# Order of the bilinear blends on VectorE: both columns of a pair, then both rows

## The chip, the cores and the metric

The kernel runs on one core of a Trainium2 chip. The metric is the device time of one execution in microseconds (us). Before the change it is 6806.22 us, the median of 10 runs (6788.82 to 6811.57).

The core's engines work in parallel, each through its own instructions in a fixed order, and wait for one another by semaphores: TensorE (PE in the profile; PEld are its weight loads), VectorE (DVE), ScalarE (ACT), GpSimd (POOL) and SyncE (SP). GpSimd issues the indirect transfers here, SyncE most of the plain ones.

## The reference

An image batch x of shape (4, 256, 64, 64), float32, goes through one block: three modulated deformable 3x3 convolutions with ReLU on the channel-normalised x, a residual, then a mixture of 8 experts (two per token) on the normalised tokens, and another residual. The change lies in the sampling of the deformable convolutions:

```python
def _bilinear(feat, ys, xs):
    y0 = jnp.floor(ys)
    x0 = jnp.floor(xs)
    wy = (ys - y0)[:, None]
    wx = (xs - x0)[:, None]
    ...
    return v00 * (1 - wy) * (1 - wx) + v01 * (1 - wy) * wx + v10 * wy * (1 - wx) + v11 * wy * wx

def _deform_layer(x, w_off, b_off, w, b, dilation=1):
    om = lax.conv_general_dilated(x, w_off, ...) + b_off[None, :, None, None]
    off = om[:, :2 * K].reshape(B, K, 2, H, W)
    mask = jax.nn.sigmoid(om[:, 2 * K:])
    ...
    sampled = _bilinear(x, ys, xs) * mask[:, None]
    wk = w.reshape(w.shape[0], w.shape[1], K)
    out = jnp.einsum('bikhw,oik->bohw', sampled, wk) + b[None, :, None, None]
    return out
```

Every output position has K = 9 taps, and every tap is one bilinear sample of all 256 channels at a position that the offset convolution gives.

## The kernel before

**Tiling.** An image is cut into 8 blocks of 512 positions (4 groups of 128). Three layers times four images make 12 stages; in each the loop of `main_block` runs over 8 blocks, 9 taps and 2 pairs of groups. A pair is two samples of 128 positions by 256 channels. That makes 12 x 8 x 9 x 2 = 1728 pairs and 3456 samples.

**One sample** (`samples`, lines 494 to 519). GpSimd issues an indirect transfer (L503) that gathers, for each of 128 positions, the four corner pixels with 256 channels each, from a table in DRAM into a tile `g` of shape 128 x 2 x 2 x 256. VectorE blends twice. L509, called the columns here, blends the two corners of each of the two columns (512 numbers a partition, with one coefficient of `cf`, in place in `g`). L514, called the rows, blends the two results across (256 numbers, with another coefficient), out of `g` into a tile `s`. The second reads what the first has just written. ScalarE then scales `s` with the third coefficient, which holds the mask and the corner weight (L517).

**One pair further** (`turn`, `finish`). Two pairs later in the program (`LAG = 2`), TensorE transposes the pair's two samples by 128x128 blocks into `tp` (L532), ScalarE copies them to `sT` (L535), and once both pairs of a tap are there, TensorE multiplies them by the tap's weights into `acc` (L555).

**Buffers.** `g` has 10 buffers (`GB`), given back when the rows are blended. `s` has 8 (`smp`), given back when the sample is transposed. A gather or a blend of rows whose buffer is not free waits, and all that stands behind it on its engine waits too.

**Work beside it.** `step` and `pump` put the other work between the taps in pieces: the offset convolution and the sampling plan of the next layer (`off_block`, L357 to L427), the normalisation of the next image (`pre_block`, L442 to L467; its last operation on VectorE is L78), tokens and routing, and the experts (`expert`, L840 to L874, with weights fetched by L800 and tokens by L812; `products` L892; `combine` L915 and L930; `give` L948).

**What sets the order.** The program is not run as written: at build time a scheduler runs a model of the program and fixes each engine's order by readiness and by place in the program. Where the author wants an order, `after(x)` adds the condition that the instructions traced inside it are issued behind `x` on the same engine. `self.last` holds the newest blend of rows, and work beside it on VectorE is often put behind that one.

Of the kernel before, what the change touches and what calls it, by code (L numbers as in the profile page):

```python
# [11 lines left out]
ALU = mybir.AluOpType  # L12
# [105 lines left out]
class Weave:  # L118
# [375 lines left out]
    def samples(self, i, n, k, t0, plan):  # L494


        nc = self.nc
        idx, cf = plan
        ss = []
        for t in (t0, t0 + 1):  # L500
            j = t * K + k
            g = self.gat.tile([P, 2, 2, C], F32, tag="g", name=f"g_{i}_{n}_{j}")
            self.gathered = nc.gpsimd.indirect_dma_start(  # L503
                out=g.rearrange("p x s f -> p (x s f)"),
                out_offset=None,
                in_=self.table(*self.stages[i]),
                in_offset=bass.IndirectOffsetOnAxis(ap=idx[:, j : j + 1], axis=0),
            )
            nc.vector.scalar_tensor_tensor(  # L509
                g[:, :, 0, :], g[:, :, 1, :], cf[:, j, 0:1], g[:, :, 0, :],  # L510
                ALU.mult, ALU.add,
            )
            s = self.smp.tile([P, C], F32, tag="s", name=f"s_{i}_{n}_{j}")
            self.last = nc.vector.scalar_tensor_tensor(  # L514
                s, g[:, 1, 0, :], cf[:, j, 1:2], g[:, 0, 0, :], ALU.mult, ALU.add
            )
            nc.scalar.activation(s, s, AF.Copy, scale=cf[:, j, 2:3])  # L517
            ss.append(s)
        return ss
# [616 lines left out]
```

## Time and profile before

| what | value |
| --- | --- |
| median of 10 runs | 6806.22 us |
| the profiled execution | 6797.38 us |
| its span, first to last instruction | 6795.6 us |
| mean granted clock of TensorE | 0.978 |
| columns, L509: count, busy, mean | 3456, 2558.8 us, 742 ns |
| rows, L514: count, busy, mean | 3456, 1659.9 us, 482 ns |
| scale, L517 (ScalarE): count, busy, mean | 3456, 1642.0 us, 508 ns |
| copy to sT, L535 (ScalarE): count, busy, mean | 1728, 1001.3 us, 586 ns |
| gather, L503 (GpSimd): count, busy, mean | 3456, 3646.5 us, 1055 ns |
| products, L555 (TensorE): count, busy | 6912, 3383.4 us |
| transposes, L532 (TensorE): count, busy | 6912, 1255.2 us |
| DMA, gathers and other indirect transfers | 1947.35 MB, 77.9% of 16 engines' span |

The busy shares of the engines over the span, in 40 equal slices (each digit in tenths, 9 is 90% or more):

```profile
PE   7998888889999999999999999999998899988987
DVE  7887778778999676668889777677778555688521
ACT  3554555555555445445555444545554444454322
POOL 4664766666667666666667777666666666677643
DMA  8998999999999999999998999989998888899744
```

The busy time of an engine counts only work; time in which it stands at a wait is idle, and the profile names what ended it. The chain of waits goes back from the last instruction, at each step to what released it or to the instruction ahead of it on its engine; its shares tell which engine's work lay on the path that set the end. A matmul's end is modelled, so a busy TensorE may still hold small gaps.

### The profile page before, as it was taken

The numbers are of one execution on the slowest core, as the hardware profiler recorded it, in microseconds if no ns is written. First come the engines' busy times: TensorE is split into PE (matmuls) and PEld (weight loads), VectorE is DVE, ScalarE is ACT, GpSimd is POOL, SyncE is SP. The second block draws the span as 40 slices with busy tenths as digits, with TensorE's granted clock in tenths as the row PEclk, the third lists the DMA queues.
The fourth block names the chain that finished last, engine by engine and source line by source line (L and its number), as shares of the span: only waits on it lengthen the run. The fifth ranks groups of instructions, "written<-read, shape, count | busy, mean of one in ns | idle before, by whom it ended". The sixth has DMA issues, their size and how long they took to land.

```text
span 6795.6 us, 88985 instructions
## 1 busy us (share of the span) xinstructions
PE 6215.6 (91%) x26500; PEld 3527.7 (52%) x26500; DVE 4961.4 (73%) x11467; ACT 3283.2 (48%) x7141; POOL 4443.5 (65%) x4245
## 2 busy tenths in 40 slices
PE   7998888889999999999999999999998899988987
PEld 3443344444445555555554545555555566755675
DVE  7887778778999676668889777677778555688521
ACT  3554555555555445445555444545554444454322
POOL 4664766666667666666667777666666666677643
PEclk8999999999999999999999999999999999999998
DMA  8998999999999999999998999989998888899744
GB/s 290 349 352 300 367 354 369 357 349 388 382 393 351 330 349 336 321 338 347 356 364 309 357 355 383 320 326 344 346 341 325 282 287 276 291 350 339 249 138 125
DMA packets 800319, 2223.73 MB, mean 327 GB/s; under 512 B 104728, under 2 KB 302872, under 8 KB 794080
## 3 DMA queue, kind: packets, MB, share of 16 engines
q0 software_dynamic: 551200, 1947.35, 77.9%
q1 hardware_dynamic: 248640, 270.69, 11.8%
q8 instruction: 215, 3.52, 0.2%
q14 instruction: 264, 2.16, 0.1%
HBM read 2160.68 MB, written 196.40 MB: 347 GB/s over the span
## 4 chain that ended last, share of the span: by engine, by line
PE 71%; ACT 8%; DMA 6%; DVE 6%; issue 4%; POOL 3%; SPq 0%; ACTq 0%; DVEq 0%; POOLq 0%
PE acc L555 36%; PE tp L532 10%; PE ph L856 7%; PE py L874 7%; PE po L357 7%; DMA g<-tab,idx 5%; ACT sT L535 3%; DVE g L509 2%; ACT s L517 2%; DVE s L514 2%; POOL gy L915 1%; POOL g L503 1%; PE pm L371 1%; PE ftp L840 1%; ACT win L577 1%
## 5 line engine op out<-in xcount | busy, mean ns | idle before, releaser
L503 POOL DMA_INDIRECT g<-tab,idx x3456 | 3646.5, 1055 | 1803.7 <-DVE s L514 655.0
L555 PE MATMUL acc<-sT,wk 128*128 128x512 f32 x6912 | 3383.4, 603 | 151.8 <-ACT sT L535 137.1
L509 DVE SCALAR_TENSOR_TENSOR g<-g,cf 128x512 f32<-128x512 f32 x3456 | 2558.8, 742 | 404.4 <-DMA g<-tab,idx 400.3
L514 DVE SCALAR_TENSOR_TENSOR s<-g,cf 128x256 f32<-128x256 f32 x3456 | 1659.9, 482 | 751.0 <-PE tp L532 466.9
L535 ACT COPY sT<-tp 128x512 f32<-128x512 f32 x1728 | 1001.3, 586 | 1823.8 <-PE tp L532 1819.1
L517 ACT ACTIVATE s<-s,cf 128x256 f32<-128x256 f32 x3456 | 1642.0, 508 | 449.5 <-DVE s L514 411.5
L555 PEld LDWEIGHTS acc<-sT,wk 128*128 128x128 f32 x6912 | 1161.2, 192 | 964.9 <-issue 653.5
L532 PEld LDWEIGHTS tp<-ident,s 128*128 128x128 f32 x6912 | 882.7, 143 | 1359.9 <-issue 652.4
L532 PE MATMUL tp<-ident,s 128*128 128x128 f32 x6912 | 1255.2, 281 | 195.4 <-ACT s L517 178.7
L856 PE MATMUL ph<-fzT,w 128*128 128x256 f32 x2608 | 689.4, 397 | 56.2 <-ACT fzT L844 36.1
L874 PE MATMUL py<-w,hT 128*128 128x256 f32 x2608 | 653.6, 389 | 30.4 <-ACT hT L866 26.8
L856 PEld LDWEIGHTS ph<-fzT,w 128*128 128x128 f32 x2608 | 485.4, 197 | 184.4 <-ACT fzT L844 63.7
L874 PEld LDWEIGHTS py<-w,hT 128*128 128x128 f32 x2608 | 475.3, 192 | 162.6 <-ACT hT L866 70.0
L866 ACT ACTIVATE hT<-ph,w 128x256 f32<-128x256 f32 x652 | 282.2, 471 | 446.1 <-PE ph L856 426.9
L812 POOL DMA_INDIRECT zt<-z,tok x326 | 334.5, 1026 | 156.5 <-issue 84.9
L357 PE MATMUL po<-win,wo 128*32 128x504 f32 (+1 forms) x2304 | 354.9, 594 | 5.9 <-ACT win L301 3.6
L800 POOL DMA_INDIRECT w<-in_W,wrow x163 | 177.1, 1086 | 270.3 <-issue 101.7
L915 POOL DMA_INDIRECT gy<-ys,slots x256 | 261.6, 1022 | 102.5 <-issue 66.0
L892 DVE TENSOR_TENSOR y<-py,w 128x512 f32<-128x512 f32 x163 | 111.5, 684 | 225.8 <-PE py L874 225.8
L930 DVE SCALAR_TENSOR_TENSOR ta<-gy,cw,ta 128x256 f32<-128x256 f32 x256 | 120.4, 479 | 123.8 <-DMA gy<-ys,slots 77.7
L357 PE MATMUL po<-win_pre,wo 128*32 128x504 f32 (+1 forms) x1152 | 185.9, 622 | 2.0 <-ACT om L366 2.0
L357 PEld LDWEIGHTS po<-win,wo 128*32 128x32 f32 x2304 | 72.7, 109 | 176.0 <-issue 140.3
(154 smaller groups left out, 2929.1 us busy)
## 6 DMA issues: line engine op xcount, KB each, us to landing
tab<-hv SPq DMA_DIRECT2D x512, 128.0 KB, 7.2
g<-tab,idx POOLq DMA_INDIRECT x3456
ys<-y SPq DMA_DIRECT2D x163, 256.0 KB, 4.5
tab<-h_pre SPq DMA_DIRECT2D x128, 256.0 KB, 6.5
wk<-in_conv_w SPq DMA_DIRECT2D x99, 256.0 KB, 7.6
xc_pre<-in_x SPq DMA_DIRECT2D x32, 512.0 KB, 8.3
xr_tok<-in_x SPq DMA_DIRECT2D x32, 512.0 KB, 8.4
t<-t_tok SPq DMA_DIRECT2D x32, 512.0 KB, 6.2
```

Source lines behind the costliest of these rows:

```text
L357: nc.tensor.matmul(po[g * Q : (g + 1) * Q, :].rearrange("q (r w) -> q r w", w=W)[:, :, x0:x1], lhsT=self.wo[l][:, 3 * ky + kx, c, :], rhs= ...
L503: self.gathered = nc.gpsimd.indirect_dma_start(out=g.rearrange("p x s f -> p (x s f)"), out_offset=None, in_=self.table(*self.stages[i]), ...
L509: nc.vector.scalar_tensor_tensor(g[:, :, 0, :], g[:, :, 1, :], cf[:, j, 0:1], g[:, :, 0, :], ALU.mult, ALU.add,)
L514: self.last = nc.vector.scalar_tensor_tensor(s, g[:, 1, 0, :], cf[:, j, 1:2], g[:, 0, 0, :], ALU.mult, ALU.add)
L517: nc.scalar.activation(s, s, AF.Copy, scale=cf[:, j, 2:3])
L532: self.turned = nc.tensor.transpose(tp[:, c, u * P : (u + 1) * P], ss[u][:, c * P : (c + 1) * P], self.ident)
L535: nc.scalar.copy(self.sT[:, :, t0 * P : (t0 + 2) * P], tp)
L555: nc.tensor.matmul(acc[:, o, :], lhsT=self.wk[k][:, c, o * P : (o + 1) * P], rhs=sT[:, c, :], start=(k == 0 and c == 0), stop=(k == K - 1 ...
L812: self.nc.gpsimd.indirect_dma_start(out=zt, out_offset=None, in_=grp.zd, in_offset=bass.IndirectOffsetOnAxis(ap=grp.tok[:, j : j + 1], axi ...
L856: nc.tensor.matmul(ph[:, h, :], lhsT=w1[:, o : o + P], rhs=zT[:, c, :], start=(c == 0), stop=(c == CC - 1),)
L874: nc.tensor.matmul(py[:, u, :], lhsT=hT[h // 2][:, h % 2, u * P : (u + 1) * P], rhs=w2[:, h * C : (h + 1) * C], start=(h == 0), stop=(h == ...
L915: self.nc.gpsimd.indirect_dma_start(out=g, out_offset=None, in_=self.ys[grp.i % 3], in_offset=bass.IndirectOffsetOnAxis(ap=grp.slots[:, i, ...
```

## The change

In `samples`, the loop over the two samples of a pair is split in two. The first loop gathers and blends the columns of each sample; the second blends the rows and scales. The rows of both samples are put behind the columns of the second (`newest` is the last one that the first loop made). No operation is added or removed, and no shape changes.

```diff
-        ss = []
+        ss, gs = [], []
         for t in (t0, t0 + 1):
             j = t * K + k
             g = self.gat.tile([P, 2, 2, C], F32, tag="g", name=f"g_{i}_{n}_{j}")
...
-            nc.vector.scalar_tensor_tensor(
+            newest = nc.vector.scalar_tensor_tensor(
                 g[:, :, 0, :], g[:, :, 1, :], cf[:, j, 0:1], g[:, :, 0, :],
                 ALU.mult, ALU.add,
             )
+            gs.append((j, g))
+        for j, g in gs:
             s = self.smp.tile([P, C], F32, tag="s", name=f"s_{i}_{n}_{j}")
-            self.last = nc.vector.scalar_tensor_tensor(
-                s, g[:, 1, 0, :], cf[:, j, 1:2], g[:, 0, 0, :], ALU.mult, ALU.add
-            )
+            with self.after(newest):
+                self.last = nc.vector.scalar_tensor_tensor(
+                    s, g[:, 1, 0, :], cf[:, j, 1:2], g[:, 0, 0, :], ALU.mult, ALU.add
+                )
             nc.scalar.activation(s, s, AF.Copy, scale=cf[:, j, 2:3])
             ss.append(s)
         return ss
```

## The prediction

> **What bounds the kernel now.** I read the page's busy line and its chain first, to see whose time sets the end.
>
> ```profile
> PE 6215.6 (91%) x26500; PEld 3527.7 (52%) x26500; DVE 4961.4 (73%) x11467; ACT 3283.2 (48%) x7141; POOL 4443.5 (65%) x4245
> ...
> PE 71%; ACT 8%; DMA 6%; DVE 6%; issue 4%; POOL 3%; SPq 0%; ACTq 0%; DVEq 0%; POOLq 0%
> PE acc L555 36%; PE tp L532 10%; PE ph L856 7%; PE py L874 7%; PE po L357 7%; DMA g<-tab,idx 5%; ACT sT L535 3%; DVE g L509 2%; ACT s L517 2%; DVE s L514 2%; POOL gy L915 1%; POOL g L503 1%; PE pm L371 1%; PE ftp L840 1%; ACT win L577 1%
> ```
>
> TensorE is busy 91% of the span and holds 71% of the chain. VectorE, the engine that the change works on, holds 6%. The two blends (L509 the columns, L514 the rows) are 2% each.
>
> Second, the timeline of VectorE alone, in a stretch that happens to hold both orders (start, duration, line; x2 is two in a row):
>
> ```profile
> 2001.02 1.40 DVE L509 SCALAR_TENSOR_TENSOR g<-g,cf 128x512 f32<-128x512 f32 x2
> 2002.35 0.87 DVE L514 SCALAR_TENSOR_TENSOR s<-g,cf 128x256 f32<-128x256 f32 x2
> 2003.14 0.74 DVE L509 SCALAR_TENSOR_TENSOR g<-g,cf 128x512 f32<-128x512 f32 x1
> 2004.01 0.48 DVE L514 SCALAR_TENSOR_TENSOR s<-g,cf 128x256 f32<-128x256 f32 x1
> 2004.41 0.75 DVE L509 SCALAR_TENSOR_TENSOR g<-g,cf 128x512 f32<-128x512 f32 x1
> 2005.29 0.48 DVE L514 SCALAR_TENSOR_TENSOR s<-g,cf 128x256 f32<-128x256 f32 x1
> ```
>
> A blend that reads the operation just ahead starts 0.13 us after it (2003.14 + 0.74 = 2003.88, next at 2004.01). One that reads nothing of it starts 0.07 us before its end (2002.42 against 2002.35). The first pair, in the order that the change asks for, takes 2.20 us (2001.02 to 2003.22), the second 2.63 us (2003.14 to 2005.77). So the stall exists, and the new order removes 0.43 us a pair.
>
> Third, TensorE's waits and those of VectorE and GpSimd on this path (total us, times, longest us).
>
> ```profile
> PE tp L532 <- ACT s L517: 178.7, 278, 2.9
> PE acc L555 <- ACT sT L535: 137.1, 209, 2.1
> ...
> PE tp_pre L462 <- DVE h_pre L78: 36.5, 15, 5.3
> ```
>
> ```profile
> DVE s L514 <- PE tp L532: 466.9, 544, 5.0
> DVE g L509 <- DMA g<-tab,idx: 400.3, 274, 10.8
> ```
>
> ```profile
> POOL g L503 <- DVE s L514: 655.0, 549, 14.0
> ```
>
> TensorE's waits for a sample are for its scale on ScalarE (L517). I followed each one back in the records: if the scale began more than 0.12 us after its blend of rows had ended, ScalarE's own queue was the cause, otherwise what held the blend. Of 183 us so followed, 141 us are ScalarE's queue, 26 us a gather that landed late, 5 us a blend that itself waited for TensorE, and only 11.5 us VectorE's queue. VectorE loses more time waiting for TensorE to give back a sample buffer (466.9 us) than TensorE loses waiting for VectorE. In 558 of the 659 such waits the buffer is that of the sample eight before: the ring of 8 is full.
>
> **The change part by part.** Nothing is added or removed: 3456 blends of columns, 3456 of rows, as many scales and gathers. The gathers keep their order in the program. What moves is the first sample's blend of rows, behind the second's blend of columns, and with it the first scale.
>
> *The stall.* Counting VectorE's records, 1783 blends of rows begin 0.10 to 0.17 us after their own blend of columns with nothing between; in the median the gap is 0.133 us, against -0.081 us behind other work. That makes 1783 x 0.214 = 382 us off VectorE's queue. On the path it is little: the chain holds 81 such neighbours, 26 of them behind a blend that a late gather let go. Those 26 lose in the new order (next part), so 55 x 0.214 = 12 us are gained. The other 1702 lie under TensorE's work. The waits for the normalised block (L78, 15 times) gain too: a normalisation lies among some six blended samples with about two stalls, 15 x 0.43 = 6 us. Bounds: nothing, and 81 x 0.214 + 36.5 = 54 us.
>
> The Trainium skill speaks against this gain: "VectorE: DVE Perf Modes", section "The DRAIN you can't avoid", reports that eight chained copies took 13.88 us with a semaphore after each and the same with only one at the end. By that rule the stall would be worth nothing. The timeline above differs, 0.13 against -0.07 us, and the measurement decides.
>
> *The late gather.* Where the second sample's gather comes late, the first sample's rows now wait for it, and the second's rows wait behind them. Before, the second blend of rows ended 0.133 + 0.482 = 0.615 us after the blend of columns. Now the first's starts at -0.081 and ends at 0.401, the second's starts at 0.320 and ends at 0.802: 0.19 us later. The two scales behind each other keep that lag (two in a row take 0.91 us in the timeline). The chain enters a blend of columns from a gather 37 times (18 first, 19 second samples): 37 x 0.19 = 7 us. Bounds: nothing, and all 274 waits, 52 us.
>
> *The first sample's buffers.* Its gather buffer is free 0.45 us later (0.662 - 0.081 + 0.482 = 1.06 against 0.615 us after its columns), the second's 0.43 us earlier. The next gather but four waits for it on GpSimd, and behind it all that GpSimd issues in order: the second gather, the expert's weights (L800), tokens (L812) and results (L915). Of the 655 us, 456 us (368 waits) are ended by a first sample. What covers it: from a gather's issue to its blend pass 13 to 15 us in most stretches, since 8 of the 10 buffers are out. Where they are not (7 us around 3740 to 4080 and after 5440), GpSimd hardly waits for blends at all (2.7 us in 3738 to 4077). I take nothing; without that cover it would be 368 x 0.45 = 166 us.
>
> *ScalarE's order.* The queues are fixed at build time from a modelled run. There the first sample's blend of rows, and so its scale, is ready later by at least a blend of columns. In ScalarE's order now, 498 of 1728 first scales stand ahead of the copy (L535) of the pair before; the other 1230 stand behind it, and that copy waits for TensorE's transposes. First samples behind the copy cost TensorE 113.6 / 1230 = 0.092 us each, those ahead 9.0 / 498 = 0.018 us. If all 498 move behind, that is 498 x 0.074 = 37 us. Bounds: the copy comes earlier in those cases, which could give back 498 / 1728 of the 137.1 us that TensorE waits for it, -39 us; and if first samples wait twice as long as now, +102 us. I take 37, the row of the very position that they move to.
>
> *Sum*: -12 - 6 + 7 + 0 + 37 = +26 us. The profiled execution took 6797.4 us (span 6795.6); it lies 8.8 us under the median of 6806.2. 6797.4 + 26 + 8.8 = 6832 us, 0.4% slower.
>
> **The rivals.** *The stall is on the path.* If VectorE's relief counts wherever VectorE is nearly full (1700 to 2040 us it is busy 322 of 340) and ScalarE's order stays, the upper bound of the gain holds: 6806 - 54 = 6752 us. For it: 408 us of the chain are VectorE's. Against: only 11.5 us of TensorE's waits end there.
>
> *All hidden.* The full sample ring hides both gain and loss: 6806 us, give or take 13. The same time would come if the build put other work between the blends so that the order hardly changed; the added condition binds only the rows behind the second columns. For it: 466.9 us of waits for the ring. Against: several fixed queues must stay where they are.
>
> *The gathers slip.* The later release of the first buffer holds GpSimd, whose gathers, at 1.055 us and 0.30 us of issue, then reach TensorE late: 6806 + 166 = 6972 us. It decides only if the 13 us of lead shrink below the flight of a gather, some 5 to 8 us in the chain. For it: 368 waits. Against: eight of ten buffers out.
>
> **How the numbers follow.** Forecast, slightly slower through ScalarE's order: 0.43. Stall on the path: 0.33. All hidden: 0.17. Gathers slip: 0.07. About 0.2% (13.6 us) is what a measurement of this kernel can tell from no change, its ten runs lying between 6789 and 6812. So faster 0.33, same 0.17, slower 0.50. The forecast's own range is 6820 to 6915 (the sum with ScalarE's term between 24 and 102, and up to 17 us of the late gathers on top). The range goes from 6750, the stall on the path at its full price, to 6930, half-way into slipped gathers beyond the forecast's top; about 2 in 10 lie outside.
>
> **What would show it.** VectorE's timeline should read two columns, two rows almost throughout, with starts 0.08 us ahead of ends, and its idle time for stalls gone. In ScalarE's order the two scales of a pair should stand together, behind the copy of the pair before. TensorE's waits for L517 should grow by some tens of us, those for L535 shrink, and GpSimd's waits for L514 keep their size. The prediction is wrong if the waits for L517 shrink or stay, if the waits for the gathers' buffers grow by more than 100 us, or if VectorE's share of the chain falls from 6% to under 4% with nothing in its place.

## The result and the profile after

The changed kernel takes 6846.06 us (median of 8 runs, 6841.27 to 6855.26), the kernel before 6805.7 us (28 runs, the ten of the table above among them). The ratio is 1.0062, with a 95% interval of 1.0054 to 1.0071: slower by some 40 us (40 between the medians, 42 by the ratio), clear of the noise. The forecast was 6832 us. The profiled execution of the changed kernel took 6861.6 us (span 6859.9 us), some 16 us above its median.

The page of the changed kernel: busy time of the engines, and the chain by engine and by line (L517 is now the rows, L520 the scale, L535 the transposes, L538 the copy, L558 the products).

```profile
PE 6235.5 (91%) x26500; PEld 3555.2 (52%) x26500; DVE 4816.9 (70%) x11467; ACT 3268.8 (48%) x7141; POOL 4800.5 (70%) x4245
...
PE 66%; DMA 11%; ACT 8%; DVE 6%; issue 5%; POOL 4%; SPq 0%; POOLq 0%; ACTq 0%; DVEq 0%
PE acc L558 34%; PE tp L535 10%; DMA g<-tab,idx 9%; PE po L357 6%; PE py L877 6%; PE ph L859 6%; ACT sT L538 4%; ACT s L520 2%; DVE g L509 2%; DVE s L517 1%; POOL g L503 1%; POOL zt L815 1%; POOL gy L918 1%; PE pm L371 1%; ACT win L580 1%
```

VectorE is busy 145 us less, since its operations now overlap at their ends where they stood apart. What grew is elsewhere: GpSimd is busy 4800.5 us against 4443.5, with the same 4245 instructions, and the gathers' DMAs are 9% of the chain against 5%. The groups of the page (busy time, mean ns of one, idle time ahead and its main releaser) show where. First the kernel before:

```profile
L503 POOL DMA_INDIRECT g<-tab,idx x3456 | 3646.5, 1055 | 1803.7 <-DVE s L514 655.0
...
L509 DVE SCALAR_TENSOR_TENSOR g<-g,cf 128x512 f32<-128x512 f32 x3456 | 2558.8, 742 | 404.4 <-DMA g<-tab,idx 400.3
```

The same two after the change:

```profile
L503 POOL DMA_INDIRECT g<-tab,idx x3456 | 3946.2, 1142 | 1509.7 <-DVE s L517 511.7
...
L509 DVE SCALAR_TENSOR_TENSOR g<-g,cf 128x512 f32<-128x512 f32 x3456 | 2514.0, 744 | 927.4 <-DMA g<-tab,idx 921.2
```

A blend of columns costs the same, 742 and 744 ns. A gather's issue on GpSimd went from 1055 to 1142 ns in the mean, 300 us in all, and VectorE's waits for gathers from 400 to 921 us. The mean hides a tail. The view of line L503 gives the least, the median and the longest, in ns; before:

```profile
L503 POOL DMA_INDIRECT g<-tab,idx x3456: 940/973/4310, 91.7 to 6372.2; - x192
```

and after:

```profile
L503 POOL DMA_INDIRECT g<-tab,idx x3456: 940/974/9408, 94.4 to 6429.9; - x192
```

The median has not moved. Counted over the records, 24 gathers took over 2 us before and 104 do now; beyond these 2 us they hold 181 us against 18. The timeline around one of them, GpSimd first (start, duration):

```profile
2469.97 1.02 POOL L503 DMA_INDIRECT g<-tab,idx  x1 [0.31 <-issue]
2471.29 9.10 POOL L503 DMA_INDIRECT g<-tab,idx  x1 [0.30 <-DVE s L517]
2480.70 0.94 POOL L503 DMA_INDIRECT g<-tab,idx  x1 [0.30 <-DVE pos L399]
```

and VectorE in the same stretch:

```profile
2470.88 1.41 DVE L509 SCALAR_TENSOR_TENSOR g<-g,cf 128x512 f32<-128x512 f32 x2
2472.20 0.88 DVE L517 SCALAR_TENSOR_TENSOR s<-g,cf 128x256 f32<-128x256 f32 x2
2472.99 1.41 DVE L509 SCALAR_TENSOR_TENSOR g<-g,cf 128x512 f32<-128x512 f32 x2
...
2477.23 1.41 DVE L509 SCALAR_TENSOR_TENSOR g<-g,cf 128x512 f32<-128x512 f32 x2
2478.55 0.88 DVE L517 SCALAR_TENSOR_TENSOR s<-g,cf 128x256 f32<-128x256 f32 x2
2479.34 0.23 DVE L395 TENSOR_TENSOR pos<-pos,base 128x72 f32<-128x72 f32 x1
2479.49 0.69 DVE L895 TENSOR_TENSOR y<-py,w 128x512 f32<-128x512 f32 x1
```

VectorE goes from blend to blend, each starting 0.08 us before the one ahead ends, for 8.5 us. The gather that GpSimd began at 2471.29 ends at 2480.39, 0.96 us after the last blend (2478.55 + 0.88 = 2479.43); the shortest gathers take 0.94 us in all. So this gather's issue seems to stand for as long as the blends follow one another without a break. Call it an unbroken stretch when each blend begins before the one ahead has ended. Of the 104 long gathers 81 end 0.80 to 1.00 us after an unbroken stretch does.

Not every gather that begins in an unbroken stretch is held. Four that GpSimd began in another one, which lasts until 1054.83:

```profile
1044.12 0.94 POOL L503 DMA_INDIRECT g<-tab,idx  x1 [12.55 <-DVE s L517]
1045.36 1.02 POOL L503 DMA_INDIRECT g<-tab,idx  x1 [0.30 <-issue]
1046.69 1.80 POOL L503 DMA_INDIRECT g<-tab,idx  x1 [0.31 <-DVE s L517]
1048.80 6.99 POOL L503 DMA_INDIRECT g<-tab,idx  x1 [0.30 <-DVE s L517]
```

```profile
1044.16 1.41 DVE L509 SCALAR_TENSOR_TENSOR g<-g,cf 128x512 f32<-128x512 f32 x2
...
1053.96 0.87 DVE L517 SCALAR_TENSOR_TENSOR s<-g,cf 128x256 f32<-128x256 f32 x2
1054.75 0.22 DVE L395 TENSOR_TENSOR pos<-pos,base 128x72 f32<-128x72 f32 x1
```

The first two are issued about as quickly as any, the fourth ends 0.96 us after the stretch. Of the 396 gathers that began with more than 2 us of an unbroken stretch still to come, 56 took over 2 us.

The long ones suggested the first theory below, *held issue*: the stall that the change removes was what let GpSimd in. The Trainium skill's page "SBUF — State Buffer" (section "SBUF: two separate sides") states that a VectorE instruction with two SBUF inputs and a GpSimd instruction that reads SBUF shut each other out for the length of one instruction. The trace agrees that there is a hold, and differs in its length: 9.10 us against blends of 0.48 and 0.74 us. No run here shows whether what the page describes is what holds a gather.

TensorE's waits after the change (total us, times, longest):

```profile
PE tp L535 <- ACT s L520: 223.1, 250, 6.3
PE acc L558 <- ACT sT L538: 161.9, 288, 0.7
```

Followed back as in the prediction, the waits for a scale now come from ScalarE's queue for 131 us (141 before), from a late gather for 65 us (26 before) and from VectorE's queue for 29 us (11.5 before). So ScalarE's queue is not what grew in the waits for a scale. The waits for the copy, which ScalarE makes too, grew by 25 us.

### The profile page after: what moved, and what is told of

Same layout as the page of the kernel before. It is cut to its first block, busy times and chain, and to the rows that moved or that the text cites. A ratio compares the mean times of both kernels' runs of the same rounds, so it can differ in the third digit from the quotient of the medians.

```text
span 6859.9 us, 88744 instructions
## 1 busy us (share of the span) xinstructions
PE 6235.5 (91%) x26500; PEld 3555.2 (52%) x26500; DVE 4816.9 (70%) x11467; ACT 3268.8 (48%) x7141; POOL 4800.5 (70%) x4245
## 3 DMA queue, kind: packets, MB, share of 16 engines
q1 hardware_dynamic: 248640, 270.69, 11.8%
## 4 chain that ended last, share of the span: by engine, by line
PE 66%; DMA 11%; ACT 8%; DVE 6%; issue 5%; POOL 4%; SPq 0%; POOLq 0%; ACTq 0%; DVEq 0%
PE acc L558 34%; PE tp L535 10%; DMA g<-tab,idx 9%; PE po L357 6%; PE py L877 6%; PE ph L859 6%; ACT sT L538 4%; ACT s L520 2%; DVE g L509 2%; DVE s L517 1%; POOL g L503 1%; POOL zt L815 1%; POOL gy L918 1%; PE pm L371 1%; ACT win L580 1%
## 5 line engine op out<-in xcount | busy, mean ns | idle before, releaser
L503 POOL DMA_INDIRECT g<-tab,idx x3456 | 3946.2, 1142 | 1509.7 <-DVE s L517 511.7
L558 PE MATMUL acc<-sT,wk 128*128 128x512 f32 x6912 | 3345.9, 608 | 175.5 <-ACT sT L538 161.9
L509 DVE SCALAR_TENSOR_TENSOR g<-g,cf 128x512 f32<-128x512 f32 x3456 | 2514.0, 744 | 927.4 <-DMA g<-tab,idx 921.2
L538 ACT COPY sT<-tp 128x512 f32<-128x512 f32 x1728 | 998.3, 586 | 1842.0 <-PE tp L535 1838.9
L517 DVE SCALAR_TENSOR_TENSOR s<-g,cf 128x256 f32<-128x256 f32 x3456 | 1530.9, 478 | 441.1 <-PE tp L535 433.9
L558 PEld LDWEIGHTS acc<-sT,wk 128*128 128x128 f32 x6912 | 1200.5, 192 | 1208.1 <-issue 871.0
L520 ACT ACTIVATE s<-s,cf 128x256 f32<-128x256 f32 x3456 | 1575.4, 505 | 483.3 <-DVE s L517 454.4
L535 PEld LDWEIGHTS tp<-ident,s 128*128 128x128 f32 x6912 | 837.9, 143 | 1064.2 <-ACT s L520 551.0
L535 PE MATMUL tp<-ident,s 128*128 128x128 f32 x6912 | 1142.0, 282 | 241.9 <-ACT s L520 223.1
L859 PE MATMUL ph<-fzT,w 128*128 128x256 f32 x2608 | 659.3, 389 | 27.4 <-DMA w<-in_W,wrow 20.7
L815 POOL DMA_INDIRECT zt<-z,tok x326 | 371.5, 1140 | 156.8 <-issue 83.9
```

Source lines behind the costliest of these rows:

```text
L503: self.gathered = nc.gpsimd.indirect_dma_start(out=g.rearrange("p x s f -> p (x s f)"), out_offset=None, in_=self.table(*self.stages[i]), ...
L509: newest = nc.vector.scalar_tensor_tensor(g[:, :, 0, :], g[:, :, 1, :], cf[:, j, 0:1], g[:, :, 0, :], ALU.mult, ALU.add,)
L517: self.last = nc.vector.scalar_tensor_tensor(s, g[:, 1, 0, :], cf[:, j, 1:2], g[:, 0, 0, :], ALU.mult, ALU.add)
L535: self.turned = nc.tensor.transpose(tp[:, c, u * P : (u + 1) * P], ss[u][:, c * P : (c + 1) * P], self.ident)
L538: nc.scalar.copy(self.sT[:, :, t0 * P : (t0 + 2) * P], tp)
L558: nc.tensor.matmul(acc[:, o, :], lhsT=self.wk[k][:, c, o * P : (o + 1) * P], rhs=sT[:, c, :], start=(k == 0 and c == 0), stop=(k == K - 1 ...
```

## The experiments

Three theories. *Held issue*: as above. *Late first sample*: the first sample's rows, scale and buffer come too late because they stand behind the second's columns. *Queue order*: the fixed orders of ScalarE and TensorE became worse, which is what the prediction's largest term says. Diffs are against the changed kernel where nothing else is said; all ratios are to the kernel before on the same chip, where it took 6804 to 6805 us if nothing else is said.

**Rows swapped.** The second sample's rows run ahead of the first's, so one stall a pair is back, between the second columns and the second rows.

```diff
-        for j, g in gs:
+        for j, g in reversed(gs):
...
+            newest = self.last
             nc.scalar.activation(s, s, AF.Copy, scale=cf[:, j, 2:3])
-            ss.append(s)
+            ss.insert(0, s)
```

> The changed order with the rows of the second sample ahead of those of the first: one blend of each pair reads the operation just ahead of it again, so VectorE stands still once a pair. Held issue (VectorE without a gap holds GpSimd while it issues a gather): gathers that take over 2 us fall from some 100 to under 60, the mean of a gather from 1142 ns to 1100 or less, and the time lies between 6806 and 6846 us or lower. Late first sample (its rows, scale and gather buffer come too late): the first sample is still later by a blend of rows, so the time is 6846 us or more. Queue order (the fixed orders of ScalarE and TensorE): both scales still stand together behind the copy, the time stays within 10 us of 6846.

Measured: 6798.28 us, ratio 0.9991 (0.9982 to 1.0). 19 gathers over 2 us. The group of gathers:

```profile
L503 POOL DMA_INDIRECT g<-tab,idx x3456 | 3746.0, 1084 | 1674.0 <-DVE s L517 684.4
```

One swap takes 48 us off the changed kernel, though the first sample's rows come later still. The late first sample falls, and so does queue order as the whole of the loss: both asked for 6846 us or about that.

**No condition.** The split loops without `after(newest)`.

```diff
-            with self.after(newest):
+            if True:
                 self.last = nc.vector.scalar_tensor_tensor(
```

> The split loops without the condition that puts the rows behind the second columns. The build then goes back to columns, rows, columns, rows on VectorE. Held issue and late first sample: the time of before, 6806 us within 10 us, a gather at 1055 ns within 15 ns. Queue order: the orders of the engines differ in detail from those of before, so the time may lie up to 30 us off.

Measured: 6813.81 us, ratio 1.0013 (1.0004 to 1.0022), a gather at 1053 ns, 27 over 2 us. VectorE's order reads columns, rows, columns, rows again. It is the old kernel with small differences in the fixed orders; these are worth 9 us here. That is how far the time can move by details of the orders, without a cause that one could name.

**The stall filled.** The kernel before, with a small sum of constants between columns and rows. This diff and the next are against the kernel before.

```diff
-            nc.vector.scalar_tensor_tensor(
+            columns = nc.vector.scalar_tensor_tensor(
...
+            with self.after(columns):
+                fill = nc.vector.tensor_tensor(self.fo, self.fa, self.fb, ALU.add)
             s = self.smp.tile([P, C], F32, tag="s", name=f"s_{i}_{n}_{j}")
-            self.last = nc.vector.scalar_tensor_tensor(
+            with self.after(fill):
+                self.last = nc.vector.scalar_tensor_tensor(
```

> The kernel before, in its own order, with a small sum of two constant tiles (128x72, about 0.23 us) between the columns and the rows of each sample, so that VectorE works through what was its stall; 3456 operations more, whose result nothing reads. The rows start when they did. Held issue: gathers over 2 us grow from 24 to over 60, the mean of a gather to 1100 ns or more, and the time is 20 us or more above 6806 and above that of the kernel with the same sum behind the rows. Late first sample: nothing is later than before, 6806 us within 15 us, like the other. Queue order: both kernels with the sum move alike.

Measured: 6848.43 us, ratio 1.0066 (1.0053 to 1.0079), but with no gather over 2 us and a mean of 1054 ns.

**The same sum behind the rows.** It follows each blend of rows instead.

```diff
-            self.last = nc.vector.scalar_tensor_tensor(
+            with self.after(columns):
+                rows = nc.vector.scalar_tensor_tensor(
...
+            with self.after(rows):
+                self.last = nc.vector.tensor_tensor(self.fo, self.fa, self.fb, ALU.add)
```

> The same 3456 small sums, but behind the rows of each sample, so the stall stays empty and VectorE works 0.15 us longer a sample (0.5 ms in all). Held issue: gathers stay near 1055 ns with some 24 over 2 us; the longer queue costs up to 30 us where VectorE is full. Late first sample: the second sample is 0.15 us later, under 15 us. Queue order: as the kernel with the filled stall, within 10 us.

Measured: 6869.8 us, ratio 1.0102 (1.0086 to 1.0119), a gather at 1095 ns, 7 over 2 us.

This pair went against held issue as I had put it, and none of the three theories had its times: the two kernels lie 44 and 65 us above the kernel before and 21 us apart. With the stall filled VectorE's records show hardly a gap, yet no gather is held. Being busy is not enough, then. In both kernels a short operation of 0.23 us stands between the blends, and in the filled one the rows still wait for their own columns (0.133 us in the median), so they do not follow in an unbroken stretch. Why the sums cost 44 and 65 us is not shown; VectorE's share of the chain is 13% and 12% there, against 6% before.

**A small sum that stalls, and one that doesn't.** The changed order with one tiny operation between the second columns and the rows. In the first kernel it reads a corner of the second columns, so VectorE stands still ahead of it; in the second it reads constants (`self.fb` in place of the corner).

```diff
+        with self.after(newest):
+            newest = nc.vector.tensor_tensor(self.fo, g[:, 1, 0, 0:4], self.fa, ALU.add)
         for j, g in gs:
```

> The changed order with one small sum (128x4, written to a scratch tile that nothing reads) between the second columns and the rows; it reads a corner of what the second columns wrote, so VectorE stands still ahead of it once a pair. It makes a pair some 0.29 us longer on VectorE (0.13 us stall, 0.16 us work), 0.5 ms in all. Held issue: gathers over 2 us fall from some 100 to under 30, a gather's mean under 1100 ns, and in spite of the longer queue the time is at most 6835 us and 10 us or more below the kernel whose small sum reads constants. Late first sample: the first rows are another 0.29 us later, so 6850 us or more and above that kernel. Queue order: the two kernels have nearly the same orders, so they agree within 8 us.

> The same small sum at the same place, reading constants: VectorE does not stand still, a pair is some 0.08 us longer. GpSimd's order is the same as with the sum that stalls. Held issue: over 60 gathers take over 2 us, a gather's mean is 1120 ns or more, and the time is 6840 us or more. Late first sample: 6846 to 6860 us, below the kernel that stalls. Queue order: within 8 us of the kernel that stalls.

Measured: with the stall 6794.78 us, ratio 0.9988 (0.9979 to 0.9997), a gather at 1070 ns, 7 over 2 us. Without it 6785.4 us, ratio 0.9976 (0.9964 to 0.9988), 1095 ns, 15 over 2 us. The longest gather of the second:

```profile
L508 POOL DMA_INDIRECT g<-tab,idx x3456: 939/963/3055, 89.7 to 6351.2; - x192
```

The first kernel's time and gathers came as held issue expected, but it was to be the faster of the two by 10 us and is the slower by 9, no more than details of the orders moved above. The second went against the theory: it needs no stall. 1728 operations more on VectorE make the changed kernel 61 us faster. GpSimd's instructions stand in the same order in both, and of the 1728 first scales 289 stand ahead of the copy of the pair before with the sum and 287 without it, so these two orders do not explain the gain. So the theory has to be mended. It is not the stall as such that lets GpSimd in but any break in an unbroken stretch of large blends, a short operation included. With that the changed kernel and the six others so far agree: many gathers over 2 us where blends follow one another unbroken (104 in the changed kernel), 0 to 27 in every kernel with a break a pair. The break cuts the holds short more than it prevents them: gathers over 3 us fall from 65 to 1 with the sum of constants, but those over 1.5 us go from 142 to 199.

**Scales ahead of the copy.** To weigh queue order by itself: on ScalarE, the copy of a pair's transposes stands behind both scales of the next pair. First on the changed kernel, then on the one with swapped rows.

```diff
-            nc.scalar.activation(s, s, AF.Copy, scale=cf[:, j, 2:3])
+            self.scaled = nc.scalar.activation(s, s, AF.Copy, scale=cf[:, j, 2:3])
...
-                self.pairs.append((i, n, k, t0, wins, ss))
+                self.pairs.append((i, n, k, t0, wins, ss, self.scaled))
...
-        i, n, k, t0, wins, ss = self.pairs.pop(0)
+        i, n, k, t0, wins, ss, _ = self.pairs.pop(0)
+        ahead = self.pairs[0][-1] if self.pairs else None
...
-        nc.scalar.copy(self.sT[:, :, t0 * P : (t0 + 2) * P], tp)
+        with self.after(ahead):
+            nc.scalar.copy(self.sT[:, :, t0 * P : (t0 + 2) * P], tp)
```

> The changed kernel with one more condition on ScalarE: the copy of a pair's transposes stands behind both scales of the next pair. Queue order: TensorE's waits for a scale (223 us) fall by 100 us or more and the time falls by 30 us or more, to 6815 us or less. Held issue: the gathers still come late and a gather's mean stays at 1120 ns or more; the time stays within 15 us of 6846. Late first sample: the copies now wait for the late scales too, 6846 us or more.

> Rows swapped (one stall a pair, 6798 us), with the same condition on ScalarE. Queue order: TensorE's waits for a scale (280 us there) fall by 100 us or more and the time to 6770 us or less. Held issue alone: a gather's mean stays near 1084 ns and the time within 15 us of 6798.

Measured: 6665.77 us, ratio 0.9795 (0.9779 to 0.9811), and 6575.78 us, ratio 0.9672 (0.9658 to 0.9687). Both beat the kernel before, and the second is the best of the study on that chip. Its chain:

```profile
PE 53%; DMA 17%; DVE 17%; issue 5%; ACT 4%; POOL 4%; SPq 0%; DVEq 0%; POOLq 0%; ACTq 0%
```

The gathers of the first (107 over 2 us) and of the second (21):

```profile
L503 POOL DMA_INDIRECT g<-tab,idx x3456: 939/986/8162, 94.2 to 6238.6; - x192
```

```profile
L503 POOL DMA_INDIRECT g<-tab,idx x3456: 940/973/4585, 92.1 to 6131.4; - x192
```

Two things follow. ScalarE's order is worth more than the change in question: 180 us on the changed kernel and 223 us on the one with swapped rows. TensorE's recorded waits for a scale show little of it: they fell by 11 and 77 us, to 211.6 and 203.1 us, not by the 100 us that I expected. Those for the copy show more, 17.0 and 27.9 us against 161.9 and 130.4. And once TensorE holds less of the chain, the two orders of the blends lie further apart: 90 us between these two kernels, 48 us without the condition. Held gathers that cost more would do that; it is not shown apart.

**The condition on the kernel before, and on the small sum.** The condition alone, with the old order of the blends; and with the changed order and the sum of constants. The edits are the ones shown above, on the kernel before and on the kernel with that sum.

> The kernel before (columns, rows, columns, rows) with the condition on ScalarE alone: the copy of a pair's transposes stands behind both scales of the next pair. Queue order: most of the gain of the swapped kernel with the condition (222 us) is ScalarE's order, so 6650 us or less, and the changed order of the blends is worth less than 70 us beside it. Held issue: gathers over 2 us stay near 24, a gather's mean near 1055 ns; the two stalls a pair cost more once TensorE no longer hides them, so it is slower than the 6576 us of the swapped rows but faster than the 6666 us of the changed order, which gathers hold back.

> The changed order with the small sum of constants between the second columns and the rows, and the condition on ScalarE. Held issue, as mended (an unbroken row of large blends holds GpSimd, a short operation lets it in): gathers over 2 us stay under 30 and the time is 6590 us or less, against 6666 us without the small sum, though VectorE does 1728 operations more. Queue order alone: the small sum changes nothing, 6666 us within 15 us.

These and the first run of the next experiment fell on a chip on which the kernel before itself took 7509 us, so only their ratios to it are used: 0.9874 (0.9842 to 0.9907) for the condition alone, with 23 gathers over 2 us, and 0.961 (0.957 to 0.965) with the small sum, with 21. The condition alone is worth less than I expected (6650 us would be 0.977); the one with the small sum is within its bound (6590 us would be 0.968). These bounds come from other chips, though, and the kernel of the next experiment has ratios of 1.011 and 1.0038 on this chip and another, so the first of the two is not firm. On this chip itself the changed order of the blends with a break a pair, beside the condition, is worth 2.6 points of the kernel before, 192 us, where I had expected less than 70. That VectorE's stalls make this up is not shown: in the profile of the condition alone VectorE holds 7% of the chain, and 9% is put down to another core or an unknown queue.

**Scales behind the copy.** The prediction's own term, alone: the kernel before, with all scales of a pair behind the copy of the pair before. The edit also moves the scales two pairs further in the program.

```diff
-            nc.scalar.activation(s, s, AF.Copy, scale=cf[:, j, 2:3])
-            ss.append(s)
+            ss.append((s, cf[:, j, 2:3]))
...
+        with self.after(self.copied):
+            for s, scale in ss:
+                nc.scalar.activation(s, s, AF.Copy, scale=scale)
+        ss = [s for s, _ in ss]
...
-        nc.scalar.copy(self.sT[:, :, t0 * P : (t0 + 2) * P], tp)
+        self.copied = nc.scalar.copy(self.sT[:, :, t0 * P : (t0 + 2) * P], tp)
```

> The kernel before with the opposite condition: both scales of a pair stand behind the copy of the pair before, which puts the 498 first scales (and some second ones) that stood ahead of it behind it. VectorE's order has its stalls as before. The prediction's term for ScalarE's order: 37 us slower, 6843 us, between 6820 and 6900. Held issue: ScalarE's order was not what made the changed kernel slower; within 15 us of 6806, with a gather's mean at 1055 ns.

> The kernel before with both scales of a pair behind the copy of the pair before, once more, since the first run fell on a chip on which the kernel before itself took 7509 us. The prediction's term for ScalarE's order: between 6820 and 6900 us; the first run's ratio of 1.011 would make 6879. Held issue: if ScalarE's order was no part of the loss, within 15 us of 6806.

Measured: ratio 1.011 (1.0076 to 1.0144) on the chip just named. On another, 6828.89 us, ratio 1.0038 (1.0025 to 1.0052), 26 us, with a gather at 1057 ns and 22 over 2 us. TensorE's waits for a scale there:

```profile
PE tp L535 <- ACT s L527: 192.3, 289, 3.3
```

On this chip the order costs 26 us when all scales are moved, second ones too; the term has 37 us for the first ones alone. TensorE's waits for a scale are only 14 us longer than in the kernel before (178.7), so they do not show all of it. The change moved fewer: of the first scales, 287 still stand ahead of the copy, against 498 before.

## Why the prediction was right, and where it failed

The sign, the range and nearly the size came out (6832 forecast, 6846 measured). The sum did not come out for its reasons, so that the number lies so near is in good part luck. Of the signs that it named, VectorE's order came (two columns, two rows almost throughout), and the waits for a scale grew by 44 us. The waits for the copy grew instead of shrinking, GpSimd's waits for rows shrank instead of keeping their size, and 287 first scales still stand ahead of the copy. Two of its figures do not follow from its own numbers: for the bound of +102 us in ScalarE's order they give 498 x (2 x 0.092 - 0.018) = 83 us, and half-way from 6915 to 6972 us is 6943, not 6930.

- **VectorE's stall** exists and is gone, as the timeline shows. Its term, 12 us and 6 us, was perhaps too small. With the holds cut short by a short operation the changed order is 0.24% faster than the kernel before (0.9976), 16 us, although the scales stand later. If ScalarE's order costs up to its measured 26 us there, the stall is worth some 40 us. This is a remainder, not measured by itself. With the scales ahead the changed order with that operation is worth 2.6 points, on the other chip; how much of it is the stall is not shown.
- **The late gather** was put at 7 us with the gathers coming as they came. TensorE's waits behind late gathers grew from 26 to 65 us, and VectorE's own waits for gathers from 400 to 921 us: the gathers themselves came later.
- **The first sample's buffers: "I take nothing".** Here the prediction failed. It looked at GpSimd only for when a buffer is given back, and never asked how long GpSimd needs to issue a gather while VectorE works. Unbroken stretches of blends can hold that issue, and the kernels that break them are faster by 61 us (the short operation) and 48 us (the swapped rows): more than the whole loss of some 40 us. GpSimd's waits for rows did not grow, they fell from 655 to 512 us; but the cover that the term relied on shrank. From the end of a gather's issue to its blend of columns passed 11.8 us in the median before and 7.9 us after, and still only 9.8 us with the rows swapped, where few gathers are held. What the later release alone costs is not shown. The rival of slipped gathers named the place, but with another mechanism and a size of 166 us.
- **ScalarE's order: +37 us.** Alone, with all scales moved, it costs 26 us on one chip (1.0038) and 1.1% on the other. In the changed kernel the waits from ScalarE's queue fell from 141 to 131 us, and the waits for the copy, which were to shrink, grew from 137.1 to 161.9 us. The term that carried the forecast is at best part of the loss.
- **The Trainium skill's rule** against the gain ("VectorE: DVE Perf Modes", section "The DRAIN you can't avoid": chained operations pay no more for a semaphore) compares the same copies with and without semaphores, which no run here does. What the runs show is a blend that starts 0.133 us after the one whose result it reads and 0.081 us before the end of one that it does not read, and a small gain where the holds are cut short (0.9976).

What stays open: why some gathers in an unbroken stretch are held and most are not, why a short operation ends a hold, and how the stall's gain and ScalarE's order divide the 16 us. The moment at which a gather begins matters. Of the 396 that began with over 2 us of an unbroken stretch to come, 55 began 0.40 to 0.44 us into the first columns of a pair or 0.12 to 0.16 us into its second rows, and 39 of these took over 2 us; of the other 341 it was 17. More gather buffers were not tried.

## What to carry to other kernels

When a stall is taken out of one engine, look at what the other engines did in it: here VectorE's stalls of 0.13 us broke up the stretches of blends that can hold GpSimd's gathers. Read the longest of a group beside its mean and median, because a hold on a few instructions shows there first. And where an order on one engine is the question, try it as one condition by itself: the single condition on ScalarE's copies takes the kernel with the rows swapped from 0.9991 to 0.9672 of the kernel before, five times what the change that led to it cost.

## What the runs showed of the hardware

A gather's issue on GpSimd takes 0.94 us at the least, 0.97 us in the median, and lasted up to 9.41 us while VectorE ran scalar_tensor_tensor operations on two SBUF inputs back to back. Most gathers that began with over 2 us of this to come took no more than 2 us (340 of 396), and 81 of the 104 long ones ended 0.80 to 1.00 us after it did. An operation of 128x4 numbers a pair was enough to cut the holds short, with 15 gathers over 2 us left of 104. On VectorE, a blend of rows that reads the operation just ahead starts 0.133 us after its end in the median, one that does not 0.081 us before it.
